# A one-element memset behind the last scatter of a recurrent layer with a mixture of experts

## The chip, the cores and the metric

The kernel runs on one core of a Trainium2 chip. The time is device microseconds of one execution, as the median of several runs; lower is better. A core has five engines with instruction streams of their own: TensorE (PE in the profile, PEld for its weight loads), VectorE (DVE), ScalarE (ACT), GpSimd (POOL) and SyncE (SP). They meet through semaphores. A row whose engine carries a "q" (POOLq, SPq) is an instruction of that engine's sequencer: a register load, a branch, a wait, a drain.

## The reference

Names are shortened; the expert weights are `wg`, `wu` (8, 1024, 256) and `wd` (8, 256, 1024).

```python
def cond(x, h0, Wx, Wh, b):
    xW = jnp.einsum('ntd,dh->nth', x, Wx) + b
    def step(prev_h, xw_t):
        next_h = jnp.tanh(xw_t + prev_h @ Wh)
        return (next_h, next_h)
    _, hs = jax.lax.scan(step, h0, jnp.swapaxes(xW, 0, 1))
    return jnp.swapaxes(hs, 0, 1)

def ffn(x, gate_w, wg, wu, wd):          # 8 experts, each token goes to 2
    logits = x_flat @ gate_w.T
    top_v, top_i = jax.lax.top_k(logits, 2)
    probs = jax.nn.softmax(top_v)
    combine = jnp.einsum('tk,tke->et', probs, jax.nn.one_hot(top_i, 8))
    def body(acc, ws):
        wge, wue, wde, we = ws
        hidden = jax.nn.silu(x_flat @ wge.T) * (x_flat @ wue.T)
        return (acc + we[:, None] * (hidden @ wde.T), None)
...
x = x + ffn(cond(x, ...), ...)
```

The kernel handles `x` (2, 1024, 256) as 2048 rows of 256 values. The result is `x` plus, in each row, the two weighted expert outputs of that token.

## The kernel before

The kernel has three stages. In the first it runs the recurrence, with TensorE's small products of the state, and beside it the routing: which two experts each token takes, with what weight, and at which place of that expert's list. Rows of state and weights go to a table `rows_d` in DRAM. The output in DRAM is first filled with `x` (two DMAs at L266 and L267), so that expert results can be added to it.

The second stage is a list of units. A unit is a share of one expert's tokens, up to 512 of them in tiles of 128. GpSimd gathers the unit's rows by an indirect DMA for each tile (`gather`, L493), TensorE turns them, and then for each of eight slices of the hidden width TensorE makes the gate and up products (L759), ScalarE and VectorE form `silu(g) * u` and split it in a high and a low part, and TensorE adds the down products (L995) in an accumulator. `add_rows` (L967) ends a tile: ScalarE scales the accumulator by the token's weight into a buffer `y` (pool `yp` with four buffers, L145), and GpSimd adds `y` to the output rows by an indirect DMA that accumulates (`scatter`, L500, called at L973). So `y` is read by a DMA, and the buffer is free once that DMA has reported that it landed.

The order on each engine is that of the program: `vec`, `act` and `pool` (L64) wrap VectorE, ScalarE and GpSimd so that every instruction given through them stays where it is written. Waits are set by a framework from what each instruction reads and writes; a write to a buffer that a DMA still reads waits for that DMA.

The last unit has four tiles, of 128, 128, 128 and 80 tokens. Its tail is written out by hand (L1094 to L1101): the down products of tile after tile, each followed by its `y` and its scatter. For the very last tile, `flag` (L1098) loads a register on every engine from `flags_i`, ahead of that tile's `y`. The pools are closed at L1102.

The third stage is an overflow path under `tc.If(special[0] > 0)` (L1105): a loop over units that did not fit, which sets its own `u.rows` (L1127), and a step-by-step fallback. In the profiled execution every engine branches over it. What then follows is the end of the program, under the line of the context that opens it (L1283): SyncE waits for every DMA and every engine's semaphore, each engine executes a drain and reports to GpSimd, GpSimd releases them, clears the semaphores, and one more such round ends the span. The start of the program has a drain on each engine too (L1276).

Of the kernel before, what the change touches and what calls it, by code (L numbers as in the profile page):

```python
# [60 lines left out]
def rnn_moe(ctx, tc, xP, cP, xT, xrows, h0T, Wx, Wh, b, gw, W, out):  # L61
    nc = tc.nc
    pe = tc.keep_in_program_order
    vec, act, pool = (InOrder(tc, e) for e in (nc.vector, nc.scalar, nc.gpsimd))  # L64
# [92 lines left out]
    def y_tile(i):  # L157
        return pl.py.tile([P, 512], F32, name=f"yb{i}")
# [340 lines left out]
    def scatter(idx, y):  # L499
        return nc.gpsimd.indirect_dma_start(  # L500
            out=out[:, :], out_offset=bass.IndirectOffsetOnAxis(ap=idx, axis=0),
            in_=y, in_offset=None, compute_op=ALU.add,
        )
# [246 lines left out]
    with ExitStack() as c2:  # L750
# [35 lines left out]
        class Job:  # L786


            def __init__(j, e=None, k=None, ids=None):
                j.e, j.k, j.ids = e, k, ids  # L790
                j.w, j.raws, j.src = None, {}, None
# [25 lines left out]
        class Unit:  # L817


            def __init__(u, job, t0=0, cols=0, tiles=None, tab=None):  # L820
                u.job, u.tab, u.main = job, tab, cols > 0
                u.tiles = [] if tiles is None else tiles
                u.t0, u.cols, u.nt = t0, cols or P, max(1, -(-cols // P))
                u.width = [min(P, u.cols - i * P) for i in range(u.nt)]
                u.steps = NIC if u.main else 2
                u.hid, u.x, u.added = {}, None, []

                u.across = u.main and u.cols > P and 0 < u.cols % P <= NARROW
                u.banks = lambda: [y_tile(i) for i in range(1 if u.nt <= 2 else 2)]
# [137 lines left out]
            def add_rows(u, i, src):  # L967
                w = u.width[i]
                y = pl.yp.tile([P, D], F32, name="y")[0:w, :]
                act.activation(y, src, AF.Copy, scale=u.comb[i][0:w, :])  # L970
                if not u.main:
                    return u.spread(y)
                ins = scatter(u.idx[i][0:w, :], y).ins  # L973
                for o in u.added:
                    tc.declare_no_dep(ins, o, reason="a unit's tiles add to different rows")
                u.added.append(ins)
# [74 lines left out]
        for n in range(len(steps)):  # L1051
            i, s = steps[n]
            u = units[i]
# [45 lines left out]
        for t in range(2, MT):  # L1099
            for i in range(TAIL, NIC):  # L1100
                u.back(i, (t,), *((flag,) if (t, i) == (MT - 1, NIC - 1) else ()))  # L1101
    wctx.close()  # L1102


    with tc.If(special[0] > 0):  # L1105

        more = nc.values_load(flags_i[0:1, 1:2], min_val=0, max_val=E * SPE)
        with tc.If(more > 0), ExitStack() as c3:
# [13 lines left out]
            with tc.For_i(0, more, 1):  # L1122
# [3 lines left out]
                u = Unit(job, tab=tab)  # L1126
# [161 lines left out]
```

## Time and profile before

| | us |
|---|---|
| median of three runs | 375.0 |
| lowest and highest of them | 374.47, 375.95 |
| the profiled execution | 373.19 |
| its span, first to last instruction | 371.4 |
| TensorE busy in it | 360.4 |
| GpSimd busy in it | 122.4 |
| last scatter: issue, to landing | 362.9, 4.7 |

The span is what the trace covers; the execution's own time is 1.8 us longer. Times within the trace count from the span's start. A row of an engine or a line gives how many instructions it has ("x27"), their busy time and the mean nanoseconds of one, and after a further bar the engine's idle time before them with what ended it. Rows of a single line give the minimum, median and maximum duration in ns and the start of the first and the last. Sequencer instructions, drains among them, do not count as busy, so a drain is seen neither in the busy share nor as a step of the chain.

### The profile page before, as it was taken

The numbers are of one execution on the slowest core, as the hardware profiler recorded it, in microseconds if no ns is written. First come the engines' busy times: TensorE is split into PE (matmuls) and PEld (weight loads), VectorE is DVE, ScalarE is ACT, GpSimd is POOL, SyncE is SP. The second block draws the span as 40 slices with busy tenths as digits, with TensorE's granted clock in tenths as the row PEclk, the third lists the DMA queues.
The fourth block names the chain that finished last, engine by engine and source line by source line (L and its number), as shares of the span: only waits on it lengthen the run. The fifth ranks groups of instructions, "written<-read, shape, count | busy, mean of one in ns | idle before, by whom it ended". The sixth has DMA issues, their size and how long they took to land.

```text
span 371.4 us, 7262 instructions
## 1 busy us (share of the span) xinstructions
PE 360.4 (97%) x2743; PEld 344.5 (93%) x2743; DVE 221.9 (60%) x541; ACT 198.9 (54%) x458; POOL 122.4 (33%) x133
## 2 busy tenths in 40 slices
PE   8999999999999999999999999999999999999990
PEld 7999999999998899999999999999999999999890
DVE  6858737786777566745547554657556546653410
ACT  5775667634756455554455445655464564463420
POOL 3794001211874223860253403341042051015041
PEclk9999999999999999999999999999999999999996
DMA  8944324231483716754164334445314352004022
GB/s 275 462 173 126 109 109 116 65 85 31 85 298 86 233 36 214 150 143 127 31 147 148 50 113 136 62 130 141 113 14 131 111 143 27 2 0 53 0 32 28
DMA packets 17804, 42.11 MB, mean 113 GB/s; under 512 B 3994, under 2 KB 12242, under 8 KB 14642
## 3 DMA queue, kind: packets, MB, share of 16 engines
q1 hardware_dynamic: 11314, 32.59, 25.4%
q0 software_dynamic: 6448, 8.99, 14.4%
q8 instruction: 23, 0.38, 0.4%
q14 instruction: 19, 0.16, 0.2%
HBM read 35.15 MB, written 9.04 MB: 119 GB/s over the span
## 4 chain that ended last, share of the span: by engine, by line
PE 94%; DMA 1%; POOL 1%; ACT 1%; DVE 1%; SPq 0%; issue 0%; POOLq 0%
PE pgu_t L759 49%; PE yb L995 21%; PE pgu_t L675 10%; PE ptr L328 3%; PE ptr L385 2%; PE ptr L219 2%; PE yb L946 2%; PE pgu_t L995 2%; DMA gu_u<-in_xP_dram 1%; PE ptr L995 1%; POOL out_dram L500 1%; PE pgu_t L310 1%; DVE gu_u L57 0%; PE yb L479 0%; PE yb L433 0%
## 5 line engine op out<-in xcount | busy, mean ns | idle before, releaser
L995 PE MATMUL yb<-wd,hh 128*128 128x256 f32 (+3 forms) x496 | 84.1, 283 | 0.0
L57 DVE TENSOR_TENSOR g<-g,pgu_t 128x256 f32<-128x256 f32 (+7 forms) x96 | 49.2, 513 | 58.1 <-PE pgu_t L759 54.6
L500 POOL DMA_INDIRECT out_dram<-y,si x27 | 44.3, 1642 | 107.7 <-ACT y L57 103.1
L57 ACT CAST hh<-g 128x256 fp32r<-128x256 f32 (+7 forms) x92 | 43.9, 477 | 65.4 <-DVE g L57 64.4
L759 PE MATMUL pgu_t<-xhi,gu_g 128*128 128x256 f32 (+7 forms) x384 | 76.9, 322 | 0.0
L759 PE MATMUL pgu_t<-xhi,gu_u 128*128 128x256 f32 (+7 forms) x384 | 76.5, 321 | 0.0
L57 ACT ACTIVATE g<-pgu_t 128x256 f32<-128x256 f32 (+7 forms) x96 | 44.1, 460 | 57.0 <-PE pgu_t L759 56.9
L995 PEld LDWEIGHTS yb<-wd,hh 128*128 128x128 f32 (+3 forms) x496 | 72.4, 185 | 1.3
L759 PEld LDWEIGHTS pgu_t<-xhi,gu_u 128*128 128x128 f32 x384 | 61.0, 188 | 3.7
L759 PEld LDWEIGHTS pgu_t<-xhi,gu_g 128*128 128x128 f32 x384 | 58.6, 189 | 2.3 <-ACT xhi L57 0.2
L493 POOL DMA_INDIRECT xg<-rows_d,gi x27 | 31.2, 1154 | 57.4 <-DVE cm L872 24.3
L57 DVE TENSOR_TENSOR hl<-g,hh 128x464 fp32r<-128x464 f32 (+5 forms) x52 | 30.5, 587 | 31.4 <-ACT hh L57 31.4
L759 PE MATMUL pgu_t<-xlo,gu_u 128*128 128x256 f32 (+7 forms) x192 | 46.1, 321 | 0.0
L759 PE MATMUL pgu_t<-xlo,gu_g 128*128 128x256 f32 (+7 forms) x192 | 46.0, 321 | 0.0
L995 PE MATMUL yb<-wd,hl 128*128 128x256 f32 (+3 forms) x152 | 42.7, 281 | 0.0
L759 PEld LDWEIGHTS pgu_t<-xlo,gu_u 128*128 128x128 f32 x192 | 32.3, 188 | 1.8
L759 PEld LDWEIGHTS pgu_t<-xlo,gu_g 128*128 128x128 f32 x192 | 32.3, 188 | 1.8
L675 PE MATMUL pgu_t<-h,wh 128*128 128x128 f32 (+1 forms) x224 | 29.1, 265 | 0.0
L995 PEld LDWEIGHTS yb<-wd,hl 128*128 128x128 f32 (+3 forms) x152 | 27.8, 183 | 0.0
L57 DVE TENSOR_TENSOR hh<-g,hh 128x256 fp32r<-128x256 f32 (+1 forms) x40 | 17.0, 424 | 17.5 <-ACT hh L57 17.4
L57 DVE TENSOR_TENSOR gu_u<-raw,gu_u 128x1024 fp32r<-128x1024 f32 (+1 forms) x18 | 20.8, 1156 | 0.6 <-ACT gu_u L57 0.6
L57 DVE TENSOR_TENSOR wd<-raw,wd 128x1024 fp32r<-128x1024 f32 (+1 forms) x18 | 19.9, 1106 | 0.9 <-ACT wd L57 0.9
(179 smaller groups left out, 480.4 us busy)
## 6 DMA issues: line engine op xcount, KB each, us to landing
raw<-in_W_dram SPq DMA_DIRECT2D x24, 1024.0 KB, 5.0
gu_u<-in_xP_dram SPq DMA_DIRECT2D x8, 256.0 KB, 4.2
rows_d<-gu_u SPq DMA_DIRECT2D x4, 320.0 KB, 3.1
rows_d<-gu_u SPq DMA_DIRECT2D x4, 192.0 KB, 2.8
out_dram<-in_xrows_dram SPq DMA_DIRECT2D x1, 512.0 KB, 17.3
xg<-rows_d,gi POOLq DMA_INDIRECT x27, 3.3
out_dram<-y,si POOLq DMA_INDIRECT x27, 3.9
small<-in_cP_dram SPq DMA_DIRECT2D x1, 267.0 KB
```

The lines of the kernel that those rows point to most:

```text
L57: return lambda *a, **k: self.tc.keep_in_program_order(f(*a, **k))
L219: pe(nc.tensor.transpose(pt[:, m, j, :], tiles[i][:, k * (P + E) : k * (P + E) + P], ident))
L310: pe(nc.tensor.matmul(bq(acc[s % 2][j])[:, :, sh:64], lhsT=wx16[:, k, j * P : (j + 1) * P], rhs=bq(x16[n][:, k, s % 2 * P : (s % 2 + 1) * ...
L328: pe(nc.tensor.matmul(pt, lhsT=wxs[a][:, k, j * P : (j + 1) * P], rhs=xparts[q % 2][c][:, k, :], start=(i == 0), stop=(i == len(terms) - 1)))
L385: pe(nc.tensor.matmul(pt[:, k * P : (k + 1) * P + E], lhsT=hall[k][:, r, :], rhs=ig[:, k, :], start=(k == 0), stop=(k == 1), skip_group_ch ...
L493: nc.gpsimd.indirect_dma_start(out=xg, out_offset=None, in_=rows[:, :], in_offset=bass.IndirectOffsetOnAxis(ap=idx, axis=0),)
L500: return nc.gpsimd.indirect_dma_start(out=out[:, :], out_offset=bass.IndirectOffsetOnAxis(ap=idx, axis=0), in_=y, in_offset=None, compute_ ...
L675: pe(nc.tensor.matmul(acc[s % 2][j], lhsT=w[:, k, j * P : (j + 1) * P], rhs=prev[k], start=False, stop=True, skip_group_check=True))
L759: pe(nc.tensor.matmul(pt, lhsT=a[i], rhs=b[j], start=(first and i + j + n == 0), stop=(j == 1 and n == len(lhs_rhs) - 1), skip_group_check ...
L946: pe(nc.tensor.matmul(yt, lhsT=wd[b][:, s, d * P : (d + 1) * P], rhs=u.hid[s][a], start=(s == 0 and n == 0), stop=(s == NIC - 1 and n == 2 ...
L995: pe(nc.tensor.matmul(yt[0:w, :], lhsT=h[a][:, i * P : i * P + w], rhs=wd[b][:, ic, :], start=(ic == 0 and first and n == 0), stop=(ic == ...
```

## The change

The buffer `y` of the last scattered rows is kept in the unit, and after the loop over the last unit's tiles GpSimd sets one element of it to zero. This is GpSimd's last instruction that is not the sequencer's own ahead of the branch over the overflow path and the drain at the end. The scatter from `y` reads the buffer before; nothing reads it afterwards.

```diff
@@ -823,7 +823,7 @@
                 u.steps = NIC if u.main else 2
-                u.hid, u.x, u.added = {}, None, []
+                u.hid, u.x, u.added, u.rows = {}, None, [], None
@@ -970,6 +970,7 @@
                 if not u.main:
                     return u.spread(y)
+                u.rows = y
                 ins = scatter(u.idx[i][0:w, :], y).ins
@@ -1099,6 +1100,8 @@
                 u.back(i, (t,), *((flag,) if (t, i) == (MT - 1, NIC - 1) else ()))
+
+        pool.memset(u.rows[0:1, 0:1], 0.0)
     wctx.close()
```

## The prediction

> **What bounds the kernel now.** I read the page's busy rows and its chain first, then the last twelve microseconds.
>
> ```profile
> span 371.4 us, 7262 instructions
> PE 360.4 (97%) x2743; PEld 344.5 (93%) x2743; DVE 221.9 (60%) x541; ACT 198.9 (54%) x458; POOL 122.4 (33%) x133
> ...
> PE 94%; DMA 1%; POOL 1%; ACT 1%; DVE 1%; SPq 0%; issue 0%; POOLq 0%
> ```
>
> TensorE carries 94% of the chain that ended last. The change adds nothing to TensorE and sits behind its last matmul, so the body of the kernel is left alone; all that can move is the tail. The chain of the last stretch (start, length, what) shows where that tail begins:
>
> ```profile
> 360.90 1.56 POOL out_dram L500
> 362.46 0.25 issue
> 362.71 0.69 POOLq L1098
> 363.41 0.96 POOL out_dram L500
> ```
>
> The last scatter is issued at 362.95 (length 1.42) and leaves GpSimd at 364.37. No engine computes after that, yet the span ends at 371.4: 7.0 us of tail. The sequencers' own instructions of the program's end (L1283; count, then min/median/max ns, then first and last start) say who is late. First from 360 to 370 us, then from 364 us on for GpSimd:
>
> ```profile
> L1283 SPq EVENT_SEMAPHORE  x12: 27/28/28, 365.0 to 368.3; - x12
> L1283 SPq DRAIN  x2: 7/10/13, 368.4 to 368.4; - x2
> L1283 POOLq DRAIN  x1: 6808/6808/6808, 363.8 to 363.8; - x1
> L1283 PEldq DRAIN  x1: 8/8/8, 364.9 to 364.9; - x1
> L1283 ACTq DRAIN  x1: 8/8/8, 365.2 to 365.2; - x1
> ```
>
> ```profile
> L1283 POOLq EVENT_SEMAPHORE  x4: 17/17/17, 370.6 to 371.3; - x4
> L1283 POOLq DRAIN  x3: 46/113/6808, 363.8 to 371.1; - x3
> ```
>
> TensorE has passed its drain at 364.9, ScalarE at 365.2, and SyncE, which waits for every DMA first, at 368.4. GpSimd's drain starts at 363.8, lasts 6.81 us and ends at 370.6; the closing round of semaphores follows within 0.8 us. So **GpSimd's drain is the last to arrive, by 2.1 us**. Was it waiting for the last scatter? These two answers bear on that (the issue from 362.5 us on with its time to landing; then the tail by windows, with the DMA share and GB/s as last columns):
>
> ```profile
> out_dram<-y,si POOLq DMA_INDIRECT x1, 4.7
> ```
>
> ```profile
> 364.37:366.60 2.23, 0.00 (x0) 0.00 (x0) 0.00 (x0) 0.00 (x0) 0.00 (x1) 0.57 0.40 53
> 366.60:367.65 1.05, 0.00 (x0) 0.00 (x0) 0.00 (x0) 0.00 (x0) 0.00 (x0) 0.50 0.00 0
> 367.65:370.57 2.92, 0.00 (x0) 0.00 (x0) 0.00 (x0) 0.00 (x0) 0.00 (x0) 0.50 0.00 0
> 370.57:371.40 0.83, 0.00 (x0) 0.00 (x0) 0.00 (x0) 0.00 (x0) 0.00 (x0) 0.50 0.00 0
> ```
>
> The scatter has landed 4.7 us after its issue, at 362.95 + 4.7 = 367.65. No byte moves after 366.6. Still the drain goes on for 2.92 us after the landing. Waiting for data does not explain these 2.92 us; something else in the drain is long, and what it is decides the sign of this change. Two more rows bear on it, the first drain of the program with a memset beside it, and the DMAs that GpSimd issued between that drain and the long one:
>
> ```profile
> L1276 POOL MEMSET const-float32-0.0<- x1: 98/98/98, 0.2 to 0.2; 128x1 f32 x1
> ...
> L1276 POOLq DRAIN  x1: 188/188/188, 0.3 to 0.3; - x1
> ```
>
> ```profile
> L500 POOL DMA_INDIRECT out_dram<-y,si x27 | 44.3, 1642 | 107.7 <-ACT y L57 103.1 <-issue 2.7 <-ACT hh L57 0.9
> L493 POOL DMA_INDIRECT xg<-rows_d,gi x27 | 31.2, 1154 | 57.4 <-DVE cm L872 24.3 <-DVE g L57 14.5 <-PE pgu_t L759 13.7
> L500 POOL DMA_INDIRECT out_dram<-y,sidx x8 | 13.7, 1713 | 13.0 <-ACT y L57 11.1 <-issue 0.6 <-ACT hh L57 0.6
> ...
> L493 POOL DMA_INDIRECT xg<-rows_d,gidx x8 | 8.0, 1005 | 17.5 <-DVE place L57 7.2 <-DVE inv L57 5.2 <-DVE eq_e L57 3.6
> ```
>
> Drains with no DMA issued ahead of them take 46, 113 and 188 ns. The long one has 27 + 27 + 8 + 8 = 70 indirect DMAs behind it.
>
> **The change part by part.** *Keeping `y`* (`u.rows = y`, and `None` at the start) is bookkeeping while the program is built: no instruction, 0 us. In the overflow path `u.rows` is set to another tile before the unit gathers, and that branch issues nothing in this trace (no instruction on L1107); 0 us.
>
> *The memset itself* is one GpSimd instruction on one element. Nearest row: 128x1 at 98 ns. A lower price for one partition is possible, a gain is not; I take 0.1 us.
>
> *The wait it brings.* It writes a buffer that the last scatter still reads, so it may start only when that DMA has reported its landing, at 367.65 instead of right behind the scatter's 364.37. A GpSimd wait for DMAs starts its next work within some 0.05 us (in the trace, the 5073 ns wait at L500 that starts at 336.9 ends at 342.02, and the scatter it watched landed at 341.99). So the memset ends at 367.65 + 0.05 + 0.1 = 367.8. Queued behind it on GpSimd are only the branch at L1105 (57 ns), a semaphore instruction (17 ns), and the drain; no DMA is queued behind it, and TensorE, VectorE and ScalarE do not read its buffer again. Who waits for the drain is every engine, in the closing round.
>
> The 4.7 us is the dearest of this kernel's last four scatters (3.9 to 4.7, median 4.1; the median of all issues of this kind is 3.9). With 3.9 the memset would end at 367.0.
>
> A rule of the Trainium skill gives less: "DMA: Bandwidth & Descriptors", section "Anatomy of one DMA — SWDGE (gpsimd) path", puts such a DMA at about 2.0 us plus its bytes at 436 GB/s. For 80 rows of 1 KB that is an estimate of 2.0 + 0.2 = 2.2 us, a landing at 365.15 and a memset that ends at 365.3, 0.9 us after the scatter left GpSimd instead of 3.4. The row of this very DMA says 4.7 us; I use the row.
>
> *The drain after it.* This is the unknown. GpSimd's sequencer runs ahead of its engine (the drain was picked up at 363.8, while the scatter ran until 364.37), so the drain may still begin at 363.8 in the record; what counts is from when its long part runs. Both ends:
>
> - Dear end: the 6.2 us between the scatter's end at 364.37 and the drain's end at 370.57 are work that the drain does once the engine is idle, about 6.2 / 70 = 89 ns for each indirect DMA issued since the last drain. Nothing of it is saved by having waited, and the memset pushes its start from 364.37 to 367.8: the drain ends at 374.0, **+3.4 us**. Counted from the drain's own start, the whole 6.81 us behind a memset that holds the sequencer too, it is 367.8 + 0.1 + 6.8 = 374.7, +4.1 us. With a landing after 3.9 us it is +2.6 us.
> - Cheap end: the drain is long because it was entered with a transfer in flight. Then, behind the memset, it costs what the other GpSimd drains cost (0.05 to 0.19 us) and ends by 368.0. SyncE's arrival at 368.4 is then the last: -2.1 us.
>
> Here a rule speaks against my choice. "VectorE: DVE Perf Modes", section "The DRAIN you can't avoid", says that the drains of a program's preamble and postamble are a constant of some 12 ns on all five engines. By that rule the change ends with GpSimd there at 367.8, ahead of SyncE, and the sum is -2.1 us. The row for this instruction is 6808 ns, with the rest of the tail's drains at 7 to 113 ns: the rule holds for all but this one, and so cannot price it. By the row the sum is +3.4 us. I take the dear end, because the trace shows the drain still running for 2.92 us with the DMA engines idle and the landing reported, which a wait for the transfer leaves unexplained, while work per DMA explains the length and also why the next two drains are short.
>
> *Sum.* In the profiled execution, span 371.4 + 3.4 = 374.8 us. That execution took 373.19 us in all (1.8 us around the span), and 375.0 is the median of the runs shown, 1.8 above it; the tail's change is added to the median: 375.0 + 3.4 = 378.4 us.
>
> **The rivals.**
>
> *Work that does not move, 0.22.* The drain's long part runs beside the memset's wait (the sequencer goes through its list from 363.8 and only then asks whether the engine is idle), or it is a fixed 2.9 us behind the landing. Then it ends between 370.6 and 367.8 + 2.9 = 370.7, and the time is 375.0 to 375.2, within 374.6 to 375.8 by the scatter of runs. For it: the sequencer is seen to run ahead. Against it: the first drain of the program waits for memsets that are running, so an idle engine is something a drain asks for. That the memset doesn't wait at all belongs here too: 375.1.
>
> *A drain that is short once nothing is in flight, 0.18.* The faster side. One mechanism: a slow way of looking for completion inside the drain, whose last look comes 2.92 us after the landing; the memset's wait replaces it with one that ends within 0.05 us. It decides as soon as the drain behind the memset takes under 2.8 us (370.6 - 367.8), and gains at most 370.6 - 368.5 = 2.1 us, as SyncE's chain of waits comes next. Time: 372.9, within 372.4 to 373.5. For it: the short drains of this trace all had nothing in flight. Against it: they also had no list of DMAs, and a 2.92 us step between looks is long beside the 0.05 us of the other waits.
>
> **How the numbers follow.** Forecast 0.60 at 378.4, own range 377.1 to 379.6 (from +2.6 to +4.1, and half a microsecond of scatter). With the 0.22 of no move this makes 0.82, so the range is 374.6 to 379.6 and leaves out the faster case and little else. A measurement of this kernel tells about 0.5%, 1.9 us, from no change. The faster case, 372.9, is 0.56% below, so some 0.13 of its 0.18 counts as faster and 0.05 as the same: faster 0.13, same 0.22 + 0.05 = 0.27, slower 0.60.
>
> **What would show it.** Right: a memset on GpSimd at about 367.7, a drain that ends near 374.0, 6.2 us after the memset, SyncE's last waits still at 368.4, and TensorE's last matmul still near 362.2. Wrong in the first way: the drain still ends near 370.6. Wrong in the second: it ends within 0.2 us of the memset, and SyncE is the last to arrive. Any difference ahead of 362 us would be none of these, and would mean that the added instruction has moved something that I left out.

## The result, and the profile after

The changed kernel takes 378.06 us (median of 16 runs, 375.97 to 379.92), the kernel before 375.79 (16 runs, 374.22 to 376.89). The ratio is 1.0067, 95% interval 1.0052 to 1.0082: slower by 2.5 us (the medians differ by 2.3). The profiled execution took 378.74 us. Its page, the busy rows and the chain:

```profile
span 376.9 us, 7263 instructions
PE 362.2 (96%) x2743; PEld 346.1 (92%) x2743; DVE 222.0 (59%) x541; ACT 198.6 (53%) x458; POOL 121.4 (32%) x134
...
issue 1%; POOLq 0%
```

One instruction more, on GpSimd. The chain's shares have collapsed from "PE 94%", although TensorE's work is the same. The reason is in the chain itself, in order of time (start, length, what):

```profile
366.66 3.47 issue
370.13 0.10 POOLq L1286
```

The chain starts from the last instruction that counts as work, and that is now the memset, not the scatter. Its first step back is the line of the program's end (L1286); it calls the 3.47 us ahead of that "issue" and stops, although the timeline below names the DMA that the memset waited for. A chain that shrinks to a percent says where following stopped, and nothing about the kernel.

The two spans differ by 5.5 us, more than the ratio: the last scatter leaves GpSimd at 367.28 instead of 364.37, 2.9 us later. That is not the change: the same gather starts at 200.83 before and at 203.74 after, so all 2.9 us are there long ahead of the memset, and a second profile of the unchanged kernel has that gather at 204.57 and its last scatter leaving at 368.11. The tail behind the scatter is what to compare: 371.40 - 364.37 = 7.03 before, 376.89 - 367.28 = 9.61 after, 2.6 us more (in the second profile of the kernel before it is 375.42 - 368.11 = 7.31). The parts of the tail after the change, first GpSimd's instructions in order of time, then the sequencers' own at the program's end up to 376.05, then the tail by windows (its last columns are the clock granted to TensorE, the DMA share and GB/s):

```profile
365.86 1.42 POOL L500 DMA_INDIRECT out_dram<-y,si  x1 [0.49 <-ACT y L57]
370.15 0.09 POOL L57 MEMSET y<- 1x1 f32 x1 [2.87 <-DMA out_dram<-y,si]
```

```profile
L1286 SPq EVENT_SEMAPHORE  x12: 28/28/28, 367.7 to 370.7; - x12
L1286 SPq DRAIN  x2: 7/10/13, 370.8 to 370.9; - x2
...
L1286 PEldq DRAIN  x1: 8/8/8, 367.7 to 367.7; - x1
L1286 ACTq DRAIN  x1: 8/8/8, 367.9 to 367.9; - x1
L1286 POOLq DRAIN  x1: 5922/5922/5922, 370.1 to 370.1; - x1
```

```profile
367.28:370.10 2.82, 0.00 (x0) 0.00 (x0) 0.00 (x0) 0.00 (x0) 0.00 (x0) 0.75 0.31 41
370.10:370.24 0.14, 0.00 (x0) 0.00 (x0) 0.00 (x0) 0.00 (x0) 0.09 (x1) 0.50 0.00 0
370.24:376.05 5.81, 0.00 (x0) 0.00 (x0) 0.00 (x0) 0.00 (x0) 0.00 (x0) 0.50 0.00 0
376.05:376.90 0.85, 0.00 (x0) 0.00 (x0) 0.00 (x0) 0.00 (x0) 0.00 (x0) 0.50 0.00 0
```

The memset waits 2.87 us for the scatter's landing, takes 88 ns, and then the drain still runs for 5.82 us, to 376.05, with no DMA in flight and every other engine arrived (SyncE at 370.9). Nothing in the trace is left for it to wait for, so I take these 5.82 us for work, and the memset has pushed it back. What that work is was the open question.

### The profile page after: what moved, and what is told of

Read it like the earlier page. It is cut to its first block, busy times and chain, and to the rows that moved or that the text cites. A ratio compares the mean times of both kernels' runs of the same rounds, so it can differ in the third digit from the quotient of the medians.

```text
span 376.9 us, 7263 instructions
## 1 busy us (share of the span) xinstructions
PE 362.2 (96%) x2743; PEld 346.1 (92%) x2743; DVE 222.0 (59%) x541; ACT 198.6 (53%) x458; POOL 121.4 (32%) x134
```

## The experiments

My theory was that the drain goes through a list of the indirect DMAs issued since the last drain, at 5.82 / 70 = 83 ns each. The rival was a fixed 5.8 us for a drain with any such DMA ahead of it. In what follows the drain's length is counted from the moment GpSimd's engine is idle, which is the memset's end where there is one, and else the end of the last indirect DMA's row. The landing of a DMA is the last of its completion reports in the trace. Where a kernel ran only once, its time is not compared, only its drain.

**An early drain.** The kernel before, with

```diff
+        pool.drain()
         for t, some in ((0, range(TAIL, NIC - 1)), (1, range(TAIL, TAIL + 1)), (0, (NIC - 1,)), (1, range(TAIL + 1, NIC))):
```

> The kernel before, with one more drain on GpSimd ahead of the last unit's four scatters, 66 indirect DMAs after the start, in GpSimd's idle 16 us. List theory (the drain goes through the indirect DMAs issued since the last drain, 5.82 us / 70 = 83 ns each behind the memset): the early drain takes 66 x 0.083 = 5.5 us, hidden; the last one has 4 entries, 0.3 us, and ends with the landing of the last scatter; SyncE becomes the last to arrive, 2.1 us earlier: ratio 0.9944, some 373.7 us. Fixed theory (any drain with DMAs behind it costs 5.8 us, whatever their number): the last drain is still some 6.2 us after the last scatter, ratio 1.000.

370.48 us against 373.51 in the same session, ratio 0.9919 (0.9896 to 0.9942). First the previous unit's last scatter and the early drain, then the drains of GpSimd and SyncE at the end, then the last scatter's time to landing:

```profile
339.58 1.43 POOL L500 DMA_INDIRECT out_dram<-y,si  x1 [0.30 <-issue]
L57 POOLq DRAIN  x1: 11793/11793/11793, 334.7 to 334.7; - x1
```

```profile
L1284 POOLq DRAIN  x3: 46/113/2604, 364.6 to 368.3; - x3
...
L1284 SPq DRAIN  x3: 7/7/13, 367.7 to 368.0; - x3
```

```profile
out_dram<-y,si POOLq DMA_INDIRECT x1, 3.2
```

The early drain ends at 346.48, 5.47 us after that scatter left GpSimd at 341.01, where 5.5 was expected (its 11.8 us include three scatters that were still to be issued). The last drain ends at 367.19, ahead of SyncE's arrival at 367.76, so SyncE is now the bound. The fixed theory is out. The gain, 3.0 us, is more than the expected 2.1. In the profiled execution the scatter landed 3.2 us after its issue and not 4.7, and without the drain in the way an early landing ends the tail earlier. That this makes up the difference in the other five runs as well is likely, but not shown.

**The same early drain in the changed kernel.**

> The changed kernel with the same early drain. Behind the memset nothing is in flight, so the last drain shows the price of 4 entries alone. List theory: 4 x 83 ns = 0.33 us, with perhaps 0.1 us fixed; GpSimd arrives about 0.5 us after the memset and the tail from the last scatter's landing to the end is some 1.6 us, not 6.8. Fixed theory: 5.8 us again.

```profile
370.23 0.09 POOL L57 MEMSET y<- 1x1 f32 x1 [3.58 <-DMA out_dram<-y,si]
```

```profile
L1287 POOLq DRAIN  x3: 46/113/512, 370.2 to 371.5; - x3
```

From the memset's end to the drain's end, at 370.72, there are 0.41 us: four entries and some 0.08 us fixed. SyncE arrives at 370.96, behind it. Timed in a second session:

> The changed kernel with the early drain, timed. List theory: the list is short (0.5 us measured for 4 entries), GpSimd and SyncE arrive within 0.3 us of each other, and the memset with its wait costs nothing any more: ratio to the kernel before 0.992, as with the early drain alone. If the wait had a price of its own beside the drain it pushes: 0.992 + 0.007 = 0.999.

372.88 us against 375.87, ratio 0.9918 (0.9892 to 0.9944), the same as without the memset (0.9919), to within some 0.0035. With a short list the memset and its wait cost nothing that is seen: **the change costs what it pushes back, not what it does**.

**Fewer and more DMAs.** The changed kernel, without the scatters of all units but the last (their results are missing from the output), and with 27 small gathers into a spare buffer:

```diff
+                if u is not units[-1]:
+                    return
                 ins = scatter(u.idx[i][0:w, :], y).ins
```

```diff
                     u.tiles.extend(gather(gi[:, c]) for c in sl)
+                    for c in sl if k is not None else ():
+                        nc.gpsimd.indirect_dma_start(
+                            out=dup[:, len(dups), :], out_offset=None, in_=rows_d[:, :],
...
```

> The changed kernel without the scatters of all units but the last: 31 of the 35 scatters are left out, so the expert results of those units are not added to the output; 39 indirect DMAs remain. List theory: the drain behind the memset takes 39 x 83 = 3.2 us. Fixed theory: 5.8 us. A theory that the price follows the rows moved by all DMAs also gives some 3.3 us, so this run does not tell it from the list theory.

> The changed kernel with 27 more indirect gathers of 8 values per row into a buffer that nothing reads: 97 indirect DMAs. List theory: 97 x 83 = 8.1 us for the drain behind the memset, unless the list has an upper length. Fixed theory: 5.8 us. The time of the body may change by what the added gathers delay, so the drain's own length is what counts.

The long drain of each, first with 39, then with 97:

```profile
L1288 POOLq DRAIN  x3: 46/112/3391, 366.8 to 370.8; - x3
```

```profile
L1293 POOLq DRAIN  x3: 46/113/4738, 380.4 to 385.7; - x3
```

39 DMAs take 3.29 us behind the memset, as expected. With 4 (0.41), 39 (3.29) and 70 (5.82) the points lie on 0.08 us + 0.082 us for each. 97 take 4.63, what 55 or 56 would, where 8.1 was expected: the list theory missed here. If it holds otherwise, DMAs leave the list on some other occasion. Two more kernels, one with 9 such gathers and one with 54, look for that:

> The changed kernel with 9 more indirect gathers of 8 values per row: 79 indirect DMAs. The run with 97 had a drain worth some 56, so somewhere a limit takes DMAs off the list. Below the limit the drain behind the memset takes 0.08 + 79 x 0.082 = 6.5 us; above it, less than the 5.82 of 70.

> The changed kernel with 54 more indirect gathers of 4 values per row: 124 indirect DMAs. A list that keeps growing gives 10.2 us behind the memset; one that is cut at a limit gives a length below the limit again, between 0 and some 7 us.

Their long drains, with 79 and with 124:

```profile
L1293 POOLq DRAIN  x3: 46/112/6657, 377.9 to 385.1; - x3
```

```profile
L1297 POOLq DRAIN  x3: 46/113/2166, 443.9 to 446.7; - x3
```

79 take 6.55 us (6.5 expected), 124 take 2.06, what 24 would. So the rule holds up to 79, and with 97 and 124 the drain pays for fewer DMAs than were issued. Which ones drop out, when and why stays open. Their number need not be what decides: these two kernels also issue 34 and 61 gathers in a row without a scatter between them, the one with 79 at most 16.

**Half the rows.** The changed kernel with every scatter cut to half its rows (half of the results are not added):

```diff
-                ins = scatter(u.idx[i][0:w, :], y).ins
+                h = w // 2
+                ins = scatter(u.idx[i][0:h, :], y[0:h, :]).ins
```

> The changed kernel with every scatter cut to the first half of its rows, so half of the expert results are not added to the output: 70 indirect DMAs still, but the 35 scatters move half as many rows. List theory, priced by the DMA: 5.8 us behind the memset as in the changed kernel. Priced by the row: the scatters are about half of the rows, so a quarter less, 4.4 us.

```profile
L1287 POOLq DRAIN  x3: 46/113/5922, 373.7 to 380.2; - x3
```

5922 ns, to the nanosecond as in the changed kernel. The price is by the DMA, not by its rows. Nor is it by GpSimd's instructions of any kind: the kernel with 39 DMAs has 103 of them instead of 134, and its drain fell by much more.

**The wait, or the delay?** The memset's place taken by five larger ones that wait for no DMA, and by one without a wait:

```diff
-        pool.memset(u.rows[0:1, 0:1], 0.0)
+        for _ in range(5):
+            pool.memset(z16, 0.0)
```

```diff
-        pool.memset(u.rows[0:1, 0:1], 0.0)
+        pool.memset(z16[0:1, 0:1], 0.0)
```

> The changed kernel with its memset replaced by five memsets of a 128x512 buffer that no DMA touches, 0.6 us each, 3.0 us in all: GpSimd is kept busy about as long as the landing kept it, but waits for nothing. List theory (the drain starts its list only when the engine is idle): the drain ends some 5.8 to 6.0 us behind the last memset, about 3.0 - 0.3 = 2.7 us later than before, ratio 1.007. Rival, that the wait for the DMA is the price: the drain's work runs beside the memsets, ratio 1.000.

> The changed kernel with its memset moved to one element of a buffer that no DMA touches: the instruction without the wait. All theories that put the price on the delay: ratio 1.000 (0.1 us). If one more instruction at the end, or a memset ahead of the drain, were the price: ratio 1.007.

Five: 378.32 us against 375.87, ratio 1.0065 (1.0041 to 1.0089), as slow as the change itself. One without a wait: 375.33, ratio 0.9996 (0.9979 to 1.0013). GpSimd's instructions at the end of the first, with its long drain:

```profile
366.31 1.42 POOL L500 DMA_INDIRECT out_dram<-y,si  x1 [0.49 <-ACT y L57]
367.23 2.80 POOL L57 MEMSET z<- 128x512 f16 x4
370.38 0.53 POOL L57 MEMSET z<- 128x512 f16 x1 [0.35 <-POOLq L1109]
```

```profile
L1287 POOLq EVENT_SEMAPHORE  x4: 17/17/17, 376.8 to 377.4; - x4
L1287 POOLq DRAIN  x3: 46/113/6351, 370.4 to 377.3; - x3
```

Here the scatter had landed at 369.56, before the last memset began, and the drain still ended 5.82 us after that memset. The wait for a DMA shows no price of its own; a delay of the engine's idle moment by other means does the same.

**The 0.38 us that did not fit.** In the kernel before, the drain ended 6.20 us past the scatter, in the kernel with the memset elsewhere 5.82. So I looked at the kernel before once more:

> The kernel before, unchanged. Its drain ran 6.20 us past the end of the last scatter, while five other drains follow 0.08 us + 0.082 us per indirect DMA, which gives 5.82 for 70. If the 0.38 us more belong to a drain entered with a landing under way, they come again: about 6.2. If they were of that one execution: about 5.82.

```profile
366.69 1.42 POOL L500 DMA_INDIRECT out_dram<-y,si  x1 [0.49 <-ACT y L57]
L1283 POOLq DRAIN  x3: 46/113/7039, 367.5 to 375.1; - x3
L1283 SPq DRAIN  x3: 7/7/13, 372.4 to 374.8; - x3
```

It ends 6.47 us after the scatter's end at 368.11, so neither 6.2 nor 5.82. But the scatter of this execution landed at 371.67, 3.56 us after it left GpSimd, and before at 367.65, 3.28 after (SyncE arrives 0.78 us behind the landing in both). Counted from the landing, both drains end 2.915 us later, half of 5.82. That led to a better theory: the drain goes through the list, waits until the last DMA has landed, and goes through it again. With p = 0.04 + 0.0411 n, in us, for one pass over n DMAs,

    end of the drain = max(engine idle + p, last landing) + p

One pass that runs beside the landing was the rival. A drain after 44 DMAs leaves 26 for the last one and tells the two apart:

```diff
+            if i == len(units) - 4 and s == 4:
+                pool.drain()
             if n == 21:
                 starts_check()
```

> The kernel before with one more drain on GpSimd after 44 of the 70 indirect DMAs, so 26 are left for the last one, which has no memset ahead of it. Two-pass theory (the drain goes through the list once, waits for the last landing, and goes through it again; each pass 0.04 us + 0.041 us per DMA): each pass takes 1.11 us, the landing comes later than the first pass ends, so the drain ends 1.11 us after the landing, whenever that is. One-pass theory (0.08 us + 0.082 us per DMA from the moment the engine is idle, beside the landing): it ends 2.21 us after the last scatter leaves GpSimd or with the landing, so 0.0 to 0.4 us after the landing. Time, either way about that of the drain ahead of the last four scatters, ratio 0.992 to 0.994.

```profile
L57 POOLq DRAIN  x1: 7562/7562/7562, 204.6 to 204.6; - x1
```

```profile
365.86 1.42 POOL L500 DMA_INDIRECT out_dram<-y,si  x1 [0.49 <-ACT y L57]
L1285 POOLq DRAIN  x3: 46/113/3467, 366.7 to 370.7; - x3
...
L1285 SPq DRAIN  x3: 7/7/13, 369.8 to 370.4; - x3
```

The scatter left GpSimd at 367.29 and landed at 369.06; the drain ended at 370.16, 1.10 us after the landing: two passes, not one. The added drain itself (first line) ended at 212.16; the gather ahead of it left GpSimd at 208.32 and landed at 210.30, so it too ends one pass, 1.85 us, behind the landing. The drains looked at, in us (p by the formula; a negative landing came before the engine was idle):

| kernel | n | p | landing after idle | drain ends after idle | formula |
|---|---|---|---|---|---|
| before | 70 | 2.92 | 3.28 | 6.20 | 6.20 |
| before again | 70 | 2.92 | 3.56 | 6.47 | 6.47 |
| changed | 70 | 2.92 | -0.14 | 5.82 | 5.83 |
| memset elsewhere | 70 | 2.92 | 1.80 | 5.82 | 5.83 |
| early drain, its own | 66 | 2.75 | 1.80 | 5.47 | 5.51 |
| early drain, last | 4 | 0.20 | 1.80 | 2.00 | 2.00 |
| drain after 44, its own | 44 | 1.85 | 1.98 | 3.84 | 3.83 |
| drain after 44, last | 26 | 1.11 | 1.77 | 2.87 | 2.88 |
| 39 DMAs | 39 | 1.64 | -0.14 | 3.29 | 3.29 |

The formula fits all of them within 0.04 us. The list and the passes are a picture that gives these ends; the trace does not show what the drain does inside.

This kernel's time is 373.81 us against 375.78, ratio 0.9951 (0.9930 to 0.9973), short of the expected 0.992 to 0.994. In the tail its drain arrives 0.3 us after SyncE, which is 0.001 of the ratio. The 7.6 us drain at 204.6 is not seen to cost anything in the body: the scatter behind it starts 3.3 us later than in the changed kernel's profile (213.09 against 209.75), but the next gather (225.01 against 225.00) and the last scatter (365.86 in both) do not move. By the formula this kernel gains 1.8 us where the last scatter lands after 2.92 us or later, and 2.9 us where it lands after 1.8; the measured 1.8 is at the lower end of that, and what is left of the shortfall is within the interval.

## Why the prediction was right, and which term was too large

*What bounds the kernel, and who is late:* right. The body did not change, GpSimd's drain was the last to arrive before and after, and SyncE stood where it was put: it arrives 0.78 us after the landing in both. A difference ahead of 362 us, which the prediction would have read as something moved by the memset, is there (2.9 us), but two profiles of the unchanged kernel differ by more.

*The memset and its start:* 0.1 us taken, 88 ns measured; it began 0.05 us after the landing, as taken.

*The sequencer runs ahead:* not here. The drain's record begins at 370.13, 17 ns before the memset, not at 363.8. It makes no difference to the end: the records begin 0.1 us (changed), 0.5 us (five memsets) and 0.6 us (memset elsewhere) ahead of the idle moment, and all three drains end 5.82 us behind it.

*The wait:* taken from the one profiled scatter, 3.28 us past the scatter's end. In the changed kernel's profile it was 2.82, and over all executions profiled between 1.8 and 3.6. The dear value was used although the prediction had named it the dearest of the last scatters. The estimate of 2.2 us that the prediction worked out from the Trainium skill ("DMA: Bandwidth & Descriptors", "Anatomy of one DMA — SWDGE (gpsimd) path") would have made the change +0.9 us; from issue to landing the last scatter took 3.2 to 5.0 us here, and the change cost 2.5.

*The drain:* this is the step that was mis-sized, "work that the drain does once the engine is idle ... Nothing of it is saved by having waited". The work is 5.82 us, not 6.20; the other 0.38 was the pause for the landing between the two passes. Before, the first pass ran while the scatter was landing, and only the second came after it. The change puts both behind it. So the cost is

    (2.82 + 0.05 + 0.09) - (6.20 - 5.82) = 2.96 - 0.38 = 2.58 us

in the two profiled executions, against +3.4 forecast and 2.5 by the ratio. The sum of terms was 0.8 too large, 0.46 from the landing and 0.38 from the drain.

Since the landing differs from one execution to the next, the cost does too. For a last scatter that lands L after it leaves GpSimd, the formula makes the change cost min(L, p) + 0.14 us, the 0.14 being the memset's start and length: 3.05 us at the 3.28 that the prediction used, 1.9 us where the scatter lands after 1.8. Over the 13 profiled executions in which the last scatter has all its rows, L is 1.8 to 3.6 and this gives 2.4 us on average, beside the 2.5 measured. That is an estimate, as these are 11 different programs with one or two executions each.

That 378.4 lies so near the measured 378.06 is in part luck with the base: the three runs shown had a median of 375.0, all sixteen 375.79.

*The rivals:* "work that does not move" had half of the truth. The 2.92 us behind the landing are a fixed part, as it said, but the list has to be gone through once before that, and this pass does move. "A drain that is short once nothing is in flight" is out: with nothing in flight it was 5.82 us. Its argument, that the short drains had nothing in flight, was really that they had no list, which the prediction gave as the reason against it. The Trainium skill's constant of some 12 ns for such drains ("VectorE: DVE Perf Modes", "The DRAIN you can't avoid") holds for the other engines (7 to 17 ns here). The prediction let it hold for all drains but the long one; GpSimd's short ones took 46, 113 and 188 ns, so it holds for none of GpSimd's.

## What to carry to other kernels

Look at the sequencers' drains, not only at busy rows: here they decided the last 7 us, and a drain shows neither in the busy shares nor as a step of the chain. An operation put ahead of a late fixed job costs what it delays that job by, not its own length; ask what part of the job used to run beside the wait. And a job that grows with everything done since the last time can be done once early, in an idle stretch: one more drain ahead of the last unit took 3.0 us off this kernel, one 26 DMAs before the end 1.8.

## What the runs showed of the hardware

GpSimd's drain costs about 0.08 us + 0.082 us for each indirect DMA issued since the last drain, whatever the DMA's rows (0.41 us for 4, 3.29 for 39, 5.82 for 70 and for 70 with half the rows in each scatter, 6.55 for 79). Its ends fit two passes with the wait for the last landing between them (26 DMAs with a landing at 1.77: 2.87 us; 70 with a landing at 3.28: 6.20). With 97 DMAs it took 4.63 us and with 124 only 2.06, which this rule does not give; why stays open. The time from the issue of the same last scatter to its landing varied between 3.2 and 5.0 us from one execution to the next.
